# One add for up to four listed tiles in the second layer of a relational graph network

## The chip, the cores and the metric

One Trainium2 chip, one of its cores. The metric is the time of one execution on the device in microseconds, as the median of the timed runs. The engines are named as in the profile: PE (matmuls; PEld are its weight loads), DVE (vectors), ACT (activations), POOL (here the engine that issues the gathers), SP (other DMAs). A name with q behind it is an engine's sequencer.

## The reference

A graph of 12500 nodes with 128 features and 200000 edges, sorted by their target `dst`, each of one of 10 relations. Two layers follow one another, then comes a layer norm over the sum with the input.

```python
def _rgcn_layer(x, src, dst, edge_type, w_rel, root, bias):
    N = x.shape[0]
    seg = dst * NUM_REL + edge_type
    xs = x[src]
    sums = jax.ops.segment_sum(xs, seg, num_segments=N * NUM_REL)
    cnt = jax.ops.segment_sum(jnp.ones(seg.shape, x.dtype), seg, num_segments=N * NUM_REL)
    mean = (sums / jnp.maximum(cnt, 1.0)[:, None]).reshape(N, NUM_REL, -1)
    return jnp.einsum('nrd,rdo->no', mean, w_rel) + x @ root + bias
...
edge_type = jnp.argmax(msg[:, NODE_EMB_DIM:-NODE_EMB_DIM], axis=1).astype(jnp.int32)
h = jax.nn.relu(_rgcn_layer(x, src, dst, edge_type, w_rel1, root1, b1))
return _rgcn_layer(h, src, dst, edge_type, w_rel2, root2, b2)
...
x = _layernorm(x + _L0_gnn_ref(x, node_vec, edge_weight, edge_attr_42, ...), axis=-1)
```

## The kernel before

The edges are cut into 1563 tiles of 128. For a tile, POOL gathers the 128 rows of its sources by an indirect DMA (`gathered`, L814); DVE makes a one-hot matrix of 128 edges by w nodes, in which an edge has its weight, 1/cnt, in the column of its target relative to the tile's first node (`hots`, L821); PE multiplies the two, which gives a sum of 128 features by w nodes in PSUM; and DVE adds it to a wide array in SBUF, at the column of the first node. That column is only known on the chip, so the address comes from a register.

**Layer 1** (`layer_1`) walks all tiles with 120-column one-hots (12 nodes by 10 relations; matmul L1058, add L847). While it runs, rows of h that are finished go into the gathered table, so that later tiles can sum the part of layer 2 whose sources are finished. Those sums are kept in `SD`, and the "heavy" blocks of layer 2 begin with them.

**Layer 2** (`layer_2`, L1382) has two kinds of tiles. First come 177 plain tiles, in 45 bunches of up to four; their one-hots are 12 wide, of `keyE` and `wE`. Then come 678 *listed* tiles: the edges whose source was not finished yet in layer 1, picked out and brought together by `brought_together` and `listed` (L1313) in six lists of up to 128 tiles, while the plain tiles run. `listed` turns the list on PE, makes for each tile its first node (`bB`), the gather's indices (`idxB`), the one-hots' columns (`keyB`) and weights (`wB`), and compares each tile's reach with its width by `by_tile` (L1340 and L1341: one pair of instructions for each step of the width in the list). A reach beyond the width sets a flag, and the call then goes through the general loops behind layer 2. The first nodes go from `biB` (L1346) through a DMA of ACT to the row `rowB`.

Listed tiles are sparser in nodes: a tile needs a window of 14 to 119 nodes (`width2`, in steps). They form two walks, listed tiles 0 to 488 (dense, 112 then 14 to 26 wide) and 489 to 677 (26 to 119 wide). `units` (L1384) makes bunches of up to four tiles of the same width in each walk, 182 in all: 157 of four, 9 of three, 7 of two, 9 of one. `taken_in_turns` (L1397) merges the walks: the first 40 and the last 40 tiles are of the first walk, and between them bunches of the second are taken as a running account allows, which counts 3 x width for each tile.

The loop over the bunches p sets the order on every engine. It does, for bunch p: the one-hots of bunch p+3 (`AH` = 3); the gathers of p and its matmuls (L1570) into PSUM bank p, out of five (`zy` three, `zq` two); then the adds of bunch p-2 (`BE` = 2), L1599, one for each tile:

```python
s = acc2[:, ds(offs[second, t], w)]
nc.vector.tensor_tensor(s, s, zps[q][:, j * w:(j + 1) * w], op=ALU.add)
```

`offsets` (L825, its load is L832) fetches the addresses of eight tiles by one register load of DVE's sequencer. Six buffers of eight tiles hold the gathered rows, so that POOL may be some 41 to 48 tiles ahead of PE's matmuls. Between the bunches stand, in every 12 tiles, 20 matmuls of 256 columns for a heavy block (`seen`, L1486, the tile `alone`) and their add three tiles later (L1494); and, as soon as all tiles of a block of 256 nodes are added, its `finish` (L1498): PE turns the block (L1504), DVE and ACT normalise it (`normed`, L754 to L764), SP stores it. 51 blocks are finished, the last three behind the last tile.

Of the kernel before, what the change touches and what calls it, by code (L numbers as in the profile page):

```python
# [20 lines left out]
P = 128  # L21
# [3 lines left out]
WN = 12  # L25
KW = NREL * WN
WMAX = 120
G = 16
QB = 4
GB = 6  # L30
# [37 lines left out]
def rgcn_resnorm_kernel(ctx: ExitStack, tc: tile.TileContext, x, src, dst, attr, w_rel1, root1, b1,  # L68
# [120 lines left out]
    def width2(u):  # L189

        a, b = rows_at(u, extent[u >= UX])
        w = max(row_width(r) for r in range(a, b + 1))
        assert w <= WMAX
        return w

    const = ctx.enter_context(tc.tile_pool(name="const", bufs=1))
    dram = ctx.enter_context(tc.tile_pool(name="dram", bufs=1, space=DRAM))
# [624 lines left out]
                                    op0=ALU.is_equal, op1=ALU.mult)  # L822
        return oh

    def offsets(row, t0, n, limits, ring=True):  # L825

        lims = [limits(t0 + j) for j in range(n)]
# [4 lines left out]
        vals = nc.values_load_multi_w_load_instructions(  # L832
            row, engines=[DVE], min_val=min(a for a, _ in lims), max_val=max(b for _, b in lims),
            skip_runtime_bounds_check_because="clamped to these nodes on the chip")[1]
        return [nc.s_assert_within(v, a, b, skip_runtime_bounds_check_because="clamped to these nodes on the chip")
                for v, (a, b) in zip(vals, lims)]
# [476 lines left out]
    def listed(c):  # L1313
# [20 lines left out]
        bi = comp.tile([P, 1], I32, name="biB")  # L1334
# [11 lines left out]
        nc.vector.tensor_scalar(bi[:p], b[:p, 0:1], -1.0, float(TOPN), op0=ALU.mult, op1=ALU.add)  # L1346
# [4 lines left out]
        nc.vector.tensor_copy(idxB[:, u0:u0 + p], ps[:, :p])  # L1351
# [30 lines left out]
    def layer_2():  # L1382

        def units(a, b):  # L1384
            u, r = a, []
            while u < b:
                w = width2(u)
                n = 1
                while u + n < b and n < min(QB, YB // w) and width2(u + n) == w:
                    n += 1  # L1390
                r.append((True, u, n, w))
                u += n
            return r
# [136 lines left out]
        for p in range(-AH, NB + BE):  # L1530
# [21 lines left out]
            if p < NB:  # L1552
# [14 lines left out]
                    gs[j] = g, at  # L1567
                for j in range(n):
                    g, at = gs.pop(j)
                    nc.tensor.matmul(zp[:, j * w:(j + 1) * w], g[:, at * C:(at + 1) * C], oh[:, j * w:(j + 1) * w],  # L1570
                                     start=True, stop=True)
                i = issued[p + 1]
            if flag is None and i >= NG - 28 * QB:
                assert not jobs.due
# [8 lines left out]
                    seen_in(j)  # L1583
            for q in [q for q in sorted(zps) if q <= p - (1 if p >= NB - 4 else BE)]:
                second, t0, n, w = bunches[q]
                for j in range(n):
                    t = t0 + j
                    if (second, t) not in offs:
                        if second:
                            m = min(GB2, (UX if t < UX else NT2) - t)  # L1590
                            assert {t // P, (t + m - 1) // P} <= ready
                            vals = offsets(rowB[:, t:t + m], t, m, bounds2, False)
                        else:
                            m = min(GB2, (NX if t >= T0 else T0) - t)
                            vals = offsets(rowP[:, t:t + m], t, m, bounds, False)
                        offs = {k: v for k, v in offs.items() if k[0] and (k[1] >= UX) != (t >= UX)}
                        offs.update({(second, t + d): v for d, v in enumerate(vals)})
                    s = acc2[:, ds(offs[second, t], w)]
                    nc.vector.tensor_tensor(s, s, zps[q][:, j * w:(j + 1) * w], op=ALU.add)  # L1599
                del zps[q]  # L1600
# [176 lines left out]
```

## Time and profile before

| | us |
|---|---|
| median of the 3 timed runs | 3716.18 |
| fastest and slowest of them | 3711.78, 3717.28 |
| the profiled execution | 3674.72 |
| its span, from the first instruction to the last | 3672.9 |

| engine | busy us | share of the span |
|---|---|---|
| PE | 2278.8 | 62% |
| PE's weight loads | 1884.6 | 51% |
| DVE | 2042.8 | 56% |
| ACT | 514.7 | 14% |
| POOL | 2293.4 | 62% |

The first gather of layer 2 starts at 2358.2 us; the first listed tile is gathered at 2639.9 us, the last at 3629.3 us. A group's row reads: line, engine, operation, written <- read tiles, shape and number of instructions, then busy us and the mean ns of one, then the engine's idle time just before them and what ended most of it ("remote" is a releaser that the trace doesn't name). A row of a timeline has its start, its length, the instruction and, in brackets, the idle time ahead of it. The mean granted clock of PE in this execution was 0.747.

### The profile page before, as it was taken

How to read it: one execution, taken by the hardware profiler on the slowest of the kernel's cores; microseconds unless marked ns; L12 is line 12 of the kernel's file. 1: busy time of each engine (PE TensorE's matmuls, PEld its weight loads, DVE VectorE, ACT ScalarE, POOL GpSimd, SP SyncE). 2: the span in 40 equal slices, each digit the busy share in tenths (PEclk: the TensorE clock that was granted, in tenths of full speed). 3: DMA queues.
4: the chain of work that ended last, by engine and by line, in shares of the span. 5: the costliest groups of instructions: out<-in, count | busy, mean ns of one | idle time of the engine just before them, and what ended most of it. 6: DMA issues, size and time to landing. Idle time of an engine off the chain costs nothing.

```text
span 3672.9 us, 39395 instructions
## 1 busy us (share of the span) xinstructions
PE 2278.8 (62%) x11107; PEld 1884.6 (51%) x11107; DVE 2042.8 (56%) x6834; ACT 514.7 (14%) x799; POOL 2293.4 (62%) x2430
## 2 busy tenths in 40 slices
PE   1557676767676767666667677633556567666533
PEld 0445555555555655555555555523455456555533
DVE  4646576767565756575656565438653234333344
ACT  1111121212121212121212121100000000000000
POOL 5664666666666666666666666566566666666663
PEclk7677887888888888888888877855667666776655
DMA  4553655455555555555555555531234444444321
GB/s 121 156 166 100 191 158 189 151 190 160 187 165 176 171 171 174 170 173 174 178 174 174 161 162 160 149 82 52 70 103 138 134 132 145 141 145 133 86 61 43
DMA packets 377189, 529.35 MB, mean 144 GB/s; under 512 B 56664, under 2 KB 284467, under 8 KB 376964
## 3 DMA queue, kind: packets, MB, share of 16 engines
q0 software_dynamic: 99552, 249.45, 23.7%
q1 hardware_dynamic: 249209, 264.48, 22.2%
q10 hardware_dynamic: 28203, 12.82, 1.2%
q8 instruction: 92, 1.51, 0.2%
q14 instruction: 133, 1.09, 0.1%
HBM read 372.75 MB, written 160.19 MB: 145 GB/s over the span
## 4 chain that ended last, share of the span: by engine, by line
PE 18%; DVE 12%; issue 11%; another core or an unknown queue 9%; POOL 1%; DVEq 1%; ACT 1%; DMA 0%; SPq 0%; POOLq 0%; ACTq 0%
PE alone L807 5%; PE zp L1058 4%; DVE oh L821 3%; DVE cc L1599 3%; PE zy L1570 2%; PE pf L807 2%; PE yb L915 2%; POOL g L814 1%; PE zq L1570 1%; DVE cc L847 1%; DVEq L832 1%; DVE cc L1261 1%; PE pf L1296 1%; DVE go L1249 0%
## 5 line engine op out<-in xcount | busy, mean ns | idle before, releaser
L814 POOL DMA_INDIRECT g<-XH,idxE x1386 | 1313.9, 948 | 737.8 <-issue 364.9
L1058 PEld LDWEIGHTS zp<-oh,g 128*128 128x128 f32 x5898 | 901.9, 230 | 399.0 <-DVE cc L847 177.1
L1058 PE MATMUL zp<-oh,g 128*128 128x120 f32 x5898 | 943.4, 317 | 238.5 <-DVE cc L847 135.2
L847 DVE TENSOR_TENSOR cc<-cc,zp 128x240 f32 (+1 forms) x1563 | 606.5, 388 | 791.3 <-remote 317.6
L814 POOL DMA_INDIRECT g<-YD,idxB x678 | 641.9, 947 | 348.8 <-issue 193.2
L915 PE MATMUL yb<-w,a 128*128 128x512 f32 (+1 forms) x576 | 347.9, 694 | 343.4 <-ACT ys L921 176.7
L821 DVE TENSOR_SCALAR oh<-bank,keyE,wE 128x120 f32<-128x120 f32 x1563 | 517.5, 393 | 0.0
L807 PE MATMUL alone<-cc,w 128*128 128x256 f32 (+2 forms) x920 | 302.9, 498 | 93.9 <-issue 64.1
L1570 PE MATMUL zy<-oh,g 128*128 128x12 f32 (+20 forms) x1158 | 217.6, 324 | 198.7 <-DVE cc L1599 124.2
L921 ACT ACTIVATE ys<-yb 128x512 f32<-128x512 f32 (+2 forms) x291 | 153.0, 526 | 1325.4 <-remote 534.1
L1570 PEld LDWEIGHTS zy<-oh,g 128*128 128x128 f32 x1158 | 222.4, 278 | 210.7 <-DVE cc L1599 128.4
L807 PEld LDWEIGHTS alone<-cc,w 128*128 128x128 f32 x920 | 233.7, 270 | 147.3 <-issue 75.5
L915 PEld LDWEIGHTS yb<-w,a 128*128 128x128 f32 x576 | 110.6, 239 | 377.6 <-ACT ys L921 198.3
L807 PE MATMUL pf<-cc,w 128*128 128x256 f32 (+2 forms) x1040 | 247.1, 395 | 17.1 <-issue 8.3
L814 POOL DMA_INDIRECT g<-in_x_dram,idxE x177 | 167.6, 947 | 134.9 <-PE zp L1058 62.6
L814 POOL DMA_INDIRECT g<-YD,idxE x177 | 168.4, 951 | 114.7 <-issue 59.7
L807 PEld LDWEIGHTS pf<-cc,w 128*128 128x128 f32 x1040 | 205.3, 211 | 50.8 <-issue 15.7
L776 ACT ACTIVATE cc<-zero 128x1280 f32<-128x1280 f32 x170 | 214.5, 1262 | 0.0
L1599 DVE TENSOR_TENSOR cc<-cc,zy 128x12 f32 (+22 forms) x579 | 102.5, 177 | 181.1 <-remote 87.9
L821 DVE TENSOR_SCALAR oh<-columns,keyB,wB 128x15 f32<-128x15 f32 (+26 forms) x678 | 159.6, 319 | 0.0
L754 DVE TENSOR_TENSOR cc<-pf,x 128x256 f32<-128x256 f32 (+2 forms) x52 | 21.2, 408 | 227.2 <-remote 94.2
L1570 PE MATMUL zq<-oh,g 128*128 128x15 f32 (+26 forms) x552 | 98.6, 319 | 63.6 <-issue 28.4
(257 smaller groups left out, 1567.8 us busy)
## 6 DMA issues: line engine op xcount, KB each, us to landing
SD<-cc SPq DMA_DIRECT2D x41, 1280.0 KB
cc<-SD SPq DMA_DIRECT2D x41, 1280.0 KB
YD<-ys SPq DMA_DIRECT2D x194, 256.0 KB
m<-in_edge_attr_dram SPq DMA_DIRECT2D x48, 672.0 KB
g<-XH,idxE POOLq DMA_INDIRECT x1386
YD<-ys SPq DMA_DIRECT2D x97, 128.0 KB
XH<-hb SPq DMA_DIRECT2D x44, 256.0 KB
g<-YD,idxB POOLq DMA_INDIRECT x678
```

The costliest lines, as they stand in the source:

```text
L776: nc.scalar.activation(cc[:, l, h * H:(h + 1) * H, o:o + n], zero[:, None, :n].to_broadcast([P, H, n]), AF.Copy)
L807: nc.tensor.matmul(po[:, :n], wsb[l][:, r, :], sums[:, r], start=(r == 0), stop=(w is None and r == NREL - 1))
L814: nc.gpsimd.indirect_dma_start(out=g[:, j * C:(j + n) * C], out_offset=None, in_=table, in_offset=bass.IndirectOffsetOnAxis(ap=idx, axis=0))
L821: nc.vector.tensor_scalar(oh[:, j * m:(j + 1) * m], cols[:, :m], keys[:, j:j + 1], weights[:, j:j + 1], op0=ALU.is_equal, op1=ALU.mult)
L832: vals = nc.values_load_multi_w_load_instructions(row, engines=[DVE], min_val=min(a for a, _ in lims), max_val=max(b for _, b in lims), sk ...
L847: nc.vector.tensor_tensor(s, s, z, op=ALU.add)
L915: nc.tensor.matmul(yb[:h, :m], fin_a[k][:, b * P:b * P + h], wsb[1][:, r:r + m // C, :], start=True, stop=True)
L921: nc.scalar.activation(ys[:h, :m], yb[:h, :m], AF.Copy)
L1058: nc.tensor.matmul(zp[:, o + l * KW:o + (l + 1) * KW], g[:, (slot[j] + l) * C:(slot[j] + l + 1) * C], oh[:, j * KW:(j + 1) * KW], start=Tr ...
L1261: nc.vector.copy_predicated(to[:, c - m:EW - m], go[:, c - KW:], a[:, c:])
L1570: nc.tensor.matmul(zp[:, j * w:(j + 1) * w], g[:, at * C:(at + 1) * C], oh[:, j * w:(j + 1) * w], start=True, stop=True)
L1599: nc.vector.tensor_tensor(s, s, zps[q][:, j * w:(j + 1) * w], op=ALU.add)
```

## The change

The listed tiles of a walk are put together in groups of four, two or one (`group_at`), and a group is a bunch. A group of n tiles has one window: its width is a constant (38.6 for four, 20.8 for two) over the smallest density of its rows, rounded up with some nodes on top, at most 120; where four tiles need more, two are tried, then one. A group doesn't cross a list. All one-hots of the group are as wide as the window, relative to the group's first node. The matmuls of its tiles write the same columns of PSUM, one on top of the other, and **one** DVE add brings the sum to SBUF. One register load brings the addresses of up to eight groups of the same size (`alike`), with a stride of n in `rowB`.

The 678 listed tiles then make 216 bunches (141 of four, 39 of two, 36 of one). Widths are 45 to 119 in the groups of four, 28 to 118 in those of two; the mean width of a one-hot goes from 27 to 68 columns. Pairs are the listed tiles from 572 to 645 with a few others, singles those from 646 on; both stand between groups of four of the first walk.

`listed` now needs the first node of a group instead of a tile's. PE turns the 128 values to a row, DVE takes the greatest of each group (in reversed order, so the first node) and writes it to all tiles of the group, writes `rowB` from that row itself, and PE turns the row back into a column. For this two more `yield`s stand in each list, that is two more pieces that are placed between bunches; the DMA of ACT goes.

```diff
+GROUPS = ((4, 38.6), (2, 20.8))
...
+    def group_at(u, end):
+
+        for n, m in GROUPS:
+            if u % P + n <= P and u + n <= end:
+                a, b = rows_at(u, extent[u >= UX])[0], rows_at(u + n - 1, extent[u >= UX])[1]
+                if a:
+                    w = int(m / min(dense[a * RT:(b + 1) * RT]) + 2.99)
+                    if w <= WMAX:
+                        return n, w
+        return 1, width2(u)
...
-        nc.vector.tensor_scalar(bi[:p], b[:p, 0:1], -1.0, float(TOPN), op0=ALU.mult, op1=ALU.add)
-        nc.scalar.dma_start(rowB[:, u0:u0 + p], bi[:p])
-        key = comp.tile([P, P], F32, name="keyb")
+        nc.tensor.transpose(ps[0:1, P:P + p], b[:p, 0:1], ident[:p, :p])
+        yield 1
...
+        for a, n, m in runs:
+            to = firsts[:, a:a + m * n]
+            if n == 1:
+                nc.vector.tensor_copy(to, ps[0:1, P + a:P + a + m])
+            else:
+                nc.vector.tensor_reduce(lasts[:, :m], ps[0:1, P + a:P + a + m * n].rearrange("p (m n) -> p m n", n=n), axis=AX.X, op=ALU.max)
+                nc.vector.tensor_copy(to.rearrange("p (m n) -> p m n", n=n), lasts[:, :m, None].to_broadcast([1, m, n]))
+        nc.tensor.matmul(ps[:p, 2 * P:2 * P + 1], firsts[:, :p], ident[0:1, 0:1], start=True, stop=True)
+        nc.vector.tensor_scalar(rowB[:, u0:u0 + p], firsts[:, :p], -1.0, float(TOPN), op0=ALU.mult, op1=ALU.add)
+        yield 1
+        nc.vector.tensor_copy(b[:p, 0:1], ps[:p, 2 * P:2 * P + 1])
         nc.vector.tensor_scalar(key[:p], si[:p], -1.0, b[:p, 0:1], op0=ALU.mult, op1=ALU.add)
...
-        by_tile(b[:, 2:3], [width2(u) - 0.5 for u in range(u0, u0 + p)])
+        by_tile(b[:, 2:3], [width_of[u] - 0.5 for u in range(u0, u0 + p)])
...
-                owed = min(owed + u[2] * (mean - 3 * u[3] - 125), mean)
+                owed = min(owed + u[2] * (mean - 3 * u[3] / u[2] - 125), mean)
...
-                    nc.tensor.matmul(zp[:, j * w:(j + 1) * w], g[:, at * C:(at + 1) * C], oh[:, j * w:(j + 1) * w],
-                                     start=True, stop=True)
+                    o = 0 if second else j * w
+                    nc.tensor.matmul(zp[:, o:o + w], g[:, at * C:(at + 1) * C], oh[:, j * w:(j + 1) * w],
+                                     start=not second or j == 0, stop=not second or j == n - 1)
...
-                for j in range(n):
+                for j in range(1 if second else n):
...
-                            m = min(GB2, (UX if t < UX else NT2) - t)
+                            step, m = n, alike[t]
...
-                            vals = offsets(rowB[:, t:t + m], t, m, bounds2, False)
+                            vals = offsets(rowB[:, t:t + m * n:n], t, m, bounds2, False, n)
```

DVE's order in the middle of the listed stage, before: the one-hots of the bunch three ahead (here of 16 columns, four in one row), then an address calculation of the sequencer ("ISA") and an add for each of the four tiles of the bunch two back.

```order
L821 TENSOR_SCALAR oh_95<-columns,keyB,wB 128x16 x4
L1599 ISA
L1599 TENSOR_TENSOR cc<-cc,zy_15678 128x16
L1599 ISA
L1599 TENSOR_TENSOR cc<-cc,zy_15678 128x16
L1599 ISA
L1599 TENSOR_TENSOR cc<-cc,zy_15678 128x16
L1599 ISA
L1599 TENSOR_TENSOR cc<-cc,zy_15678 128x16
```

The same engine in the same part of the program after it, where groups of four of the first walk alternate with single tiles of the second.

```order
L846 TENSOR_SCALAR oh_98<-columns,keyB,wB 128x51 x4
L1636 ISA
L1636 TENSOR_TENSOR cc<-cc,zy_15680 128x74
L846 TENSOR_SCALAR oh_92<-columns,keyB,wB 128x74
L1636 ISA
L1636 TENSOR_TENSOR cc<-cc,zq_17203 128x51
L846 TENSOR_SCALAR oh_93<-columns,keyB,wB 128x52 x4
L1636 ISA
L1636 TENSOR_TENSOR cc<-cc,zq_17204 128x74
L846 TENSOR_SCALAR oh_94<-columns,keyB,wB 128x84
L1636 ISA
L1636 TENSOR_TENSOR cc<-cc,zy_15678 128x51
```

Four pairs of address and add have become one for each group; a single tile has a one-hot, an address and an add of its own, and takes a whole turn of the loop.

DVE's order in a list, from the reduction to each tile's greatest node on (L1343), before; `biB` is what ACT's DMA takes to `rowB`, and the rows of L832 and L1599 are those of a plain bunch that follows.

```order
L1343 TENSOR_REDUCE bB<-si 128x1
L1344 TENSOR_SCALAR bB<-bB,reach_173,reach_172 128x1
L1346 TENSOR_SCALAR biB<-bB 128x1
L1349 TENSOR_SCALAR keyb<-si,bB 128x128
L832 TENSOR_LOAD rowP
L1599 ISA
L1599 TENSOR_TENSOR cc<-cc,zy_15680 128x12
```

After it, in the first list: these rows stand one bunch later than the reduction, behind the turning on PE (`pf` is its result). The first two rows belong to `brought_together`.

```order
L1315 TENSOR_SCALAR go<-columns,fB 127x7
L1317 TENSOR_TENSOR cc<-columns,go 127x896
L1384 COPY keyb<-pf 1x2
L1386 TENSOR_REDUCE dn<-pf 1x31
L1387 COPY keyb<-dn 1x124
L1386 TENSOR_REDUCE dn<-pf 1x1
L1387 COPY keyb<-dn 1x2
L1389 TENSOR_SCALAR rowB<-keyb 1x128
L1636 ISA
```

The column for the keys comes one bunch later again, as a copy of PE's second result, and only then the keys (L1392, before it L1349).

More of the change, by code (lines that the diff above doesn't have):

```diff
@@ L194, in width2 @@
         return w
+    def group_at(u, end):
[7 more added lines that the diff above has]
+        return 1, width2(u)
+    groups2, u = [], 0
+    while u < NT2:
+        n, w = group_at(u, UX if u < UX else NT2)
+        groups2.append((u, n, w))
+        u += n
+    alike = {}
+    for k, (u, n, _) in enumerate(groups2):
+        m = 1
+        while m < GB2 and k + m < len(groups2) and groups2[k + m][1] == n and (groups2[k + m][0] < UX) == (u < UX):
+            m += 1
+        alike[u] = m
+    width_of = {u + j: w for u, n, w in groups2 for j in range(n)}
     const = ctx.enter_context(tc.tile_pool(name="const", bufs=1))
@@ L823, in hots, with offsets @@
         return oh
-    def offsets(row, t0, n, limits, ring=True):
-        lims = [limits(t0 + j) for j in range(n)]
+    def offsets(row, t0, n, limits, ring=True, step=1):
+        lims = [limits(t0 + j * step) for j in range(n)]
         if ring:
@@ L1333, in listed @@
         b = comp.tile([P, 4], F32, name="bB")
-        bi = comp.tile([P, 1], I32, name="biB")
+        key = comp.tile([P, P], F32, name="keyb")
+        firsts, lasts = key[0:1], dn[0:1]
         def by_tile(to, vals):
@@ L1345, in listed @@
                                 op0=ALU.max, op1=ALU.min)
-        nc.vector.tensor_scalar(bi[:p], b[:p, 0:1], -1.0, float(TOPN), op0=ALU.mult, op1=ALU.add)
-        nc.scalar.dma_start(rowB[:, u0:u0 + p], bi[:p])
-        key = comp.tile([P, P], F32, name="keyb")
+        nc.tensor.transpose(ps[0:1, P:P + p], b[:p, 0:1], ident[:p, :p])
+        yield 1
+        runs = []
+        for u, n, _ in groups2:
+            if u0 <= u < u0 + p:
+                if runs and runs[-1][1] == n:
+                    runs[-1][2] += 1
+                else:
+                    runs.append([u - u0, n, 1])
+        for a, n, m in runs:
+            to = firsts[:, a:a + m * n]
+            if n == 1:
+                nc.vector.tensor_copy(to, ps[0:1, P + a:P + a + m])
+            else:
+                nc.vector.tensor_reduce(lasts[:, :m], ps[0:1, P + a:P + a + m * n].rearrange("p (m n) -> p m n", n=n), axis=AX.X, op=ALU.max)
[4 more added lines that the diff above has]
+        nc.vector.tensor_copy(b[:p, 0:1], ps[:p, 2 * P:2 * P + 1])
         nc.vector.tensor_scalar(key[:p], si[:p], -1.0, b[:p, 0:1], op0=ALU.mult, op1=ALU.add)
@@ L1384, in units @@
         def units(a, b):
[L1385 to L1393, printed above, removed]
+            return [(True, u, n, w) for u, n, w in groups2 if a <= u < b]
         walks = [units(0, UX), units(UX, NT2)]
@@ L1589, in layer_2 @@
                         if second:
-                            m = min(GB2, (UX if t < UX else NT2) - t)
-                            assert {t // P, (t + m - 1) // P} <= ready
-                            vals = offsets(rowB[:, t:t + m], t, m, bounds2, False)
+                            step, m = n, alike[t]
+                            assert {t // P, (t + m * n - 1) // P} <= ready
+                            vals = offsets(rowB[:, t:t + m * n:n], t, m, bounds2, False, n)
                         else:
+                            step = 1
                             m = min(GB2, (NX if t >= T0 else T0) - t)
@@ L1596, in layer_2 @@
                         offs = {k: v for k, v in offs.items() if k[0] and (k[1] >= UX) != (t >= UX)}
-                        offs.update({(second, t + d): v for d, v in enumerate(vals)})
+                        offs.update({(second, t + d * step): v for d, v in enumerate(vals)})
                     s = acc2[:, ds(offs[second, t], w)]
```

## The prediction

> **What bounds the kernel now.** I read the busy time by stretches first, because the share of an engine over the whole span is a mean over stages. In each row below stand the stretch, its length, and the busy time of PE, PE's weight loads, DVE, ACT and POOL with the number of their instructions.
>
> ```profile
> core 0: us, PE busy (x) PEld busy (x) DVE busy (x) ACT busy (x) POOL busy (x), PEclk, DMA share, GB/s
> ...
> 1600.00:2100.00 500.00, 339.28 (x1837) 275.75 (x1837) 307.78 (x858) 103.81 (x143) 323.16 (x341) 0.85 0.55 171
> ...
> 2600.00:2760.00 160.00, 100.20 (x423) 85.08 (x423) 93.70 (x436) 7.13 (x18) 90.96 (x96) 0.69 0.32 92
> ...
> 2960.00:3460.00 500.00, 328.23 (x1380) 284.26 (x1380) 188.07 (x913) 18.06 (x49) 327.37 (x346) 0.69 0.46 135
> 3460.00:3630.00 170.00, 59.15 (x275) 55.52 (x273) 60.66 (x307) 2.66 (x9) 114.51 (x122) 0.52 0.23 60
> 3630.00:3673.00 43.00, 19.82 (x85) 17.88 (x85) 24.40 (x119) 2.06 (x7) 0.22 (x1) 0.50 0.13 26
> ```
>
> POOL's gathers are one to a tile. 500/341 = 1.466 us each in layer 1, with DVE busy 62% of the time; 500/346 = 1.445 us in the listed stage, with DVE at 38%; 170/122 = 1.393 us near its end, with PE at 35% and DVE at 36%. DVE's and PE's load hardly move this pace, so POOL sets it. Only 2600:2760, where the lists are made (160/96 = 1.67 us), and the last 43 us, with one gather left, go by something else. The timeline of POOL shows how the pace comes about; in brackets is the idle time before a gather.
>
> ```profile
> 3024.74 0.95 POOL L814 DMA_INDIRECT g<-YD,idxB  x1 [3.50 <-PE pf L1504]
> ...
> 3047.95 0.94 POOL L814 DMA_INDIRECT g<-YD,idxB  x1 [3.46 <-PE zy L1570]
> ...
> 3059.61 0.95 POOL L814 DMA_INDIRECT g<-YD,idxB  x1 [1.96 <-PE zy L1570]
> ...
> 3533.44 0.94 POOL L814 DMA_INDIRECT g<-YD,idxB  x1 [4.35 <-remote]
> 3567.68 0.95 POOL L814 DMA_INDIRECT g<-YD,idxB  x1 [4.54 <-remote]
> ```
>
> 16 gathers lie between the first two rows (23.21 us, 1.451 each), 8 to the third (11.66 us, 1.458), 24 between the last two (34.24 us, 1.427). Without the pause a gather starts (23.21 - 0.95 - 3.46) / 15 = 1.253 us after the one before. The pause grows with the number of gathers before it, 2.0, 3.5 and 4.5 us, so 8, 16 or 24 at a stretch come to nearly the same pace. A stretch ends where eight buffers aren't known to be free. That depends on PE, which stands behind DVE:
>
> ```profile
> L754 DVE TENSOR_TENSOR cc<-pf,x 128x256 f32<-128x256 f32 x42 | 17.8, 424 | 210.0 <-remote 89.6 <-PE zy L1570 70.6 <-issue 23.9
> L1494 DVE TENSOR_TENSOR cc<-cc,alone 128x256 f32<-128x256 f32 x41 | 17.2, 418 | 134.1 <-remote 86.9 <-PE zy L1570 22.4 <-PE zq L1570 15.0
> ```
>
> From 2700 on, DVE idles 344 us before the 42 finished blocks and the 41 sums of the finished part, both of which need PE. It is not short of time there.
>
> **The change, part by part.** 678 listed tiles keep 678 gathers, 678 one-hots and their matmuls. Their adds become 216 (141 groups of four, 39 of two, 36 of one), the loads of their addresses 33 instead of 86.
>
> ```profile
> L821 DVE TENSOR_SCALAR oh<-columns,keyB,wB 128x15 f32<-128x15 f32 x85 | 19.2, 313 | 0.0
> ...
> L821 DVE TENSOR_SCALAR oh<-columns,keyB,wB 128x66 f32<-128x66 f32 x9 | 2.5, 356 | 0.0
> L1599 DVE TENSOR_TENSOR cc<-cc,zy 128x119 f32 x9 | 2.5, 278 | 10.1 <-DVE cc L1599 4.5 <-issue 3.8 <-remote 1.8
> ...
> L1599 DVE TENSOR_TENSOR cc<-cc,zq 128x66 f32 x8 | 1.8, 224 | 13.3 <-PE alone L807 8.9 <-remote 2.3 <-issue 1.9
> ```
>
> ```profile
> L832 DVEq TENSOR_LOAD <-rowB x86: 309/599/2106, 2705.7 to 3660.7; - x86
> ```
>
> *Beside POOL.* One add in a run takes 0.2 us (a row of the tail, below), so 462 fewer are 92 us; 53 fewer loads at 0.599 are 32 us. One-hots widen from a mean of 27 to 68 columns: at most 2.5/9 - 19.2/85 = 0.05 us each, 34 us. The 216 adds are 74 wide in the mean, between 224 and 278 ns, about 0.05 us more each: 11 us. DVE is relieved of 92 + 32 - 34 - 11 = 79 us. POOL's pace hides all of it, as 1600:2100 against 2960:3460 shows; without that cover it would be the gain of the first rival.
>
> *The steady stage: -6.* What DVE's relief can do is lengthen POOL's stretches. The last sum of a finished part is this row, and from there on the pauses come every 24 gathers instead of 16:
>
> ```profile
> 3495.37 0.29 DVE L1494 TENSOR_TENSOR cc<-cc,alone 128x128 f32<-128x128 f32 x1 [9.10 <-remote]
> ```
>
> ```profile
> L814 POOL DMA_INDIRECT g<-YD,idxB x577: 942/947/1023, 2760.7 to 3601.8; - x193
> ```
>
> So fewer stops of DVE do lengthen them, at 1.451 - 1.427 = 0.024 us a gather. From the first to the last of these 577 gathers go 841.1 us, 1.460 each; at 1.427 throughout that is -19, the near end. I take 250 gathers at -0.024, for the groups of four that follow one another at both ends of the stage (about 200 tiles) and a few more. The far end, +60, is the second rival's mechanism.
>
> *The lists: +8.* These groups are from 2600:2760, where all six lists are made:
>
> ```profile
> L1341 DVE TENSOR_TENSOR bB<-bB 128x1 f32<-128x1 f32 x30 | 4.9, 162 | 1.7 <-DVE bB L1340 0.5 <-issue 0.2
> L1340 DVE TENSOR_SCALAR bB<-place 128x1 f32<-128x1 f32 x30 | 4.6, 153 | 1.5 <-DVE bB L1341 0.7
> ...
> L1351 DVE CAST idxB<-pf 128x128 int32<-128x128 f32 (+1 forms) x6 | 1.6, 269 | 7.5 <-remote 5.8 <-PE zy L1570 1.7
> ...
> L1371 DVE COPY wB<-pf 128x128 f32<-128x128 f32 (+1 forms) x5 | 1.3, 268 | 4.5 <-PE pf L1369 4.5
> ...
> L1346 DVE TENSOR_SCALAR biB<-bB 128x1 int32<-128x1 f32 (+1 forms) x6 | 0.9, 152 | 0.2
> ```
>
> The steps of width grow from 30 pairs to 46: 32 x 0.158 = 5.1 us. 24 copies and reductions of one row, six addresses and six columns come, six L1346 go: 30 more in all, between 30 x 0.15 and 30 x 0.27, 4.5 to 8 us. Two more places per list at which DVE waits for PE: L1351 and L1371 waited 12.0 us in 11 cases, 1.1 each, so 12 x 1.1 = 13 us. Behind such a wait stand the next bunch's one-hots and the adds that free PE's banks, and PE waits for both. Together 23 to 26 us of DVE, in a stretch where DVE is idle for 66 of 160 us, and where POOL is 160 - 96 x 1.451 = 21 us behind its pace. Nothing (all in the idle time) and +25 (all in line) are the ends; I take a third. A gain is unlikely: of what goes, only six short instructions and six DMA issues of ACT, which is busy for 7 of 160 us.
>
> *The tail: -11.* After the last gather DVE goes on by itself.
>
> ```profile
> 3613.13 0.18 DVE L1599 TENSOR_TENSOR cc<-cc,zy 128x23 f32 x1 [2.01 <-remote]
> 3613.83 0.18 DVE L1599 TENSOR_TENSOR cc<-cc,zy 128x23 f32 x1 [0.52 <-DVE cc L1599]
> ...
> 3629.96 0.18 DVE L1599 TENSOR_TENSOR cc<-cc,zy 128x23 f32 x1 [6.60 <-remote]
> ...
> 3640.86 0.81 DVE L1599 TENSOR_TENSOR cc<-cc,zy 128x24 f32 x4
> ```
>
> ```profile
> L821 DVE TENSOR_SCALAR oh<-columns,keyB,wB 128x26 f32<-128x26 f32 (+1 forms) x27 | 6.1, 293 | 0.0
> ...
> L1599 DVE TENSOR_TENSOR cc<-cc,zy 128x25 f32 (+3 forms) x26 | 4.7, 180 | 11.3 <-remote 6.6 <-DVE cc L1599 3.8
> ...
> L1599 DVE TENSOR_TENSOR cc<-cc,zq 128x25 f32 (+3 forms) x22 | 3.9, 179 | 2.0 <-DVE cc L1599 1.5
> ```
>
> ```profile
> L832 DVEq TENSOR_LOAD <-rowB x6: 309/598/702, 3638.7 to 3660.7; - x6
> ```
>
> Four adds take 0.81 us there. The 26 + 22 adds become 13: 35 x 0.2 = 7.0 us less, 13 x 0.05 = 0.7 more for width; four loads at 0.598 go, 2.4 less; 27 one-hots widen, 27 x 0.05 = 1.3 more. That is -7.4. The rows at 3613 to 3630 show, while POOL still issues, single adds that wait 0.5 to 6.6 us, some of them for the add just before. With one add for four tiles DVE has fewer such waits ahead of the last gather: 0 to -8, of which I take -3.6. Ends of the tail: 0 (the closing blocks' chain of PE, DVE and ACT keeps the end) and -16.
>
> *Sum.* 8 - 6 - 11 = -9 us. Against the profiled execution, 3674.72 us (span 3672.9), that is 3665.7. The median of the timed runs, 3716.18, lies 41.5 us above that execution; the 9 us taken from it give **3707 us**.
>
> **The rivals.** *First, faster: DVE's loop with PE is what holds POOL* (0.13). For it: DVE's single adds above wait for each other while POOL issues, and a group has one. Then the steady stage gets its -19, the lists give back 16 of their 21 us, the tail -16: -51, 3665. More would need pauses to vanish altogether (576 x 0.2 = 115 us more), and layer 1's 1.466 with its different load on DVE and PE speaks against it. The Trainium skill, "Perfetto Trace Analysis", section "Optimizing Scalar/DVE Operations", says that grouping into larger operations can raise throughput if the engine is saturated; DVE's 38% in 2960:3460 is not that case.
>
> *Second, slower: the bunch shrinks* (0.25). One-hots are made three bunches ahead, PE has five banks, one to a bunch. Before, a bunch holds 678/182 = 3.7 tiles, after it 678/216 = 3.1, and where the two walks alternate (some 477 tiles in 163 bunches) 2.9: when DVE stands before a finished block, PE has 8 to 9 tiles to go on with instead of 11. POOL needs 8. Falling from 16 to 8 at a stretch costs only 0.007 a gather, 3 us; a pause that truly waits for PE costs more:
>
> ```profile
> 2879.92 0.95 POOL L814 DMA_INDIRECT g<-YD,idxB  x1 [5.28 <-PE zy L1570]
> ...
> 2955.20 0.95 POOL L814 DMA_INDIRECT g<-YD,idxB  x1 [6.60 <-PE zq L1570]
> ```
>
> Both end stretches of 8 and are 3.3 and 4.6 us over the 1.96 above. With 60 pauses in the 477 tiles and one in eight late, 7.5 x 4 = 30 us, and +30 + 8 - 11 = +27: 3743. It decides from about three late pauses on (12 us, against 17 of tail and stretches). Against it: DVE has less to do between its stops.
>
> *Third, slower: the lists in line* (0.12). All 25 us show: 25 - 6 - 11 = +8, 3724.
>
> *Fourth, slower: wide one-hots hold POOL up* (0.03). If a one-hot kept a gather from being made, 678 x 0.05 us times POOL's busy 0.65 would add 22 us: 22 + 8 - 11 = +19, 3735. In layer 1 one-hots of 120 columns run beside gathers that take no longer:
>
> ```profile
> L814 POOL DMA_INDIRECT g<-XH,idxE x1386 | 1313.9, 948 | 737.8 <-issue 364.9
> ...
> L821 DVE TENSOR_SCALAR oh<-bank,keyE,wE 128x120 f32<-128x120 f32 x1563 | 517.5, 393 | 0.0
> ```
>
> The mean is 948 ns beside 120 columns, the median 947 in the listed stage, beside 27. The Trainium skill has such a rule in "SBUF — State Buffer", section "Who interferes with whom": a tensor_scalar in a two-port mode locks GpSimd out of the shared ports and so starves descriptor generation; these rows show no sign of it.
>
> *Fifth, it doesn't do what it says* (0.02): if a group's nodes don't fit its window, the flag sends the call through the general loops, and the time is far above all of this.
>
> **How the numbers follow.** The forecast has 0.45; its own ends, +7 and -25, put 0.30 on faster and 0.15 on no change. 0.2%, or 7.4 us, is about what a measurement of this kernel can tell from none. Faster: 0.30 + 0.13 = 0.43. Same: 0.15 + 0.03 of the second rival + 0.05 of the third = 0.23. Slower: 0.22 + 0.07 + 0.03 + 0.02 = 0.34. The range goes from 3678 (two thirds of the way from the forecast to the first rival's 3665, with some 0.08 left below) to 3745 (the second rival's price, with 0.10 left above).
>
> **What would show it.** Right: the gathers of 2960:3460 stay within 340 to 352; pauses come every 24 gathers where fours follow fours; the last gather is followed by about 32 us instead of 43, with some 13 adds; DVE's busy time in the listed stage falls by about 79 us and POOL's pace doesn't follow. Wrong: more than 355 gathers in 500 us (first rival); POOL's idle time with pauses over 5 us in the middle, released by PE (second); under 92 gathers in the stretch in which the lists are made (third); gathers longer than 0.95 us (fourth).

## The result, and the profile after

The change took 3685.99 us (median of 10 runs, 3682.37 to 3700.1), the kernel before 3707.98 us (median of 10, 3702.23 to 3717.28): a ratio of 0.9946, with a 95% interval of 0.9931 to 0.996, so 0.5% or some 20 us faster. Forecast were 9 us, from 3716 us, the median of three runs; over ten runs that kernel takes 3708 us, so the forecast time of 3707 us is practically that of the kernel before.

The two profiled executions don't show this by their spans: 3681.0 us after, 3672.9 before. Layer 1, in which not one instruction is changed, ends (first gather of layer 2) at 2385.4 us after and at 2358.2 us before. The profile of before is of an execution 1.1% below its timed runs, as the prediction noted. So only layer 2 is compared: 3672.9 - 2358.2 = 1314.7 us before, 3681.0 - 2385.4 = 1295.6 us after, 19 us less.

The stretches of the kernel after, with the same columns as in the prediction:

```profile
core 0: us, PE busy (x) PEld busy (x) DVE busy (x) ACT busy (x) POOL busy (x), PEclk, DMA share, GB/s
2600.00:2760.00 160.00, 95.52 (x390) 80.87 (x390) 96.10 (x407) 7.37 (x17) 90.62 (x96) 0.67 0.29 81
2960.00:3460.00 500.00, 319.45 (x1350) 271.28 (x1351) 157.22 (x683) 19.45 (x51) 324.55 (x344) 0.70 0.46 135
3460.00:3630.00 170.00, 71.50 (x363) 67.63 (x362) 56.67 (x252) 2.95 (x10) 112.64 (x120) 0.56 0.26 68
3653.00:3681.00 28.00, 11.86 (x53) 10.52 (x52) 14.81 (x63) 1.77 (x6) 1.36 (x2) 0.50 0.23 37
```

In 500 us of the listed stage DVE is busy for 157 us instead of 188, with 683 instructions instead of 913, and POOL makes 344 gathers instead of 346. DVE's relief is there and POOL's pace doesn't follow it. What is shorter is the end: from the last gather to the last instruction 3681.0 - 3653.7 = 27.3 us, against 3672.93 - 3629.28 = 43.7.

Where did DVE's saved time go? These are the adds of the listed tiles and the two other places at which DVE stops, from 2840 to 3620 us before, with busy time, mean and idle time ahead of them:

```profile
L1599 DVE TENSOR_TENSOR cc<-cc,zy 128x15 f32 (+20 forms) x320 | 58.6, 183 | 98.3 <-issue 33.5 <-remote 32.7 <-DVE cc L1599 25.3
L1599 DVE TENSOR_TENSOR cc<-cc,zq 128x15 f32 (+21 forms) x219 | 41.0, 187 | 63.9 <-remote 16.3 <-issue 14.2 <-DVE cc L1599 14.1
L754 DVE TENSOR_TENSOR cc<-pf,x 128x256 f32<-128x256 f32 (+2 forms) x38 | 15.8, 417 | 194.0 <-remote 76.4 <-PE zy L1570 69.1 <-issue 23.9
L1494 DVE TENSOR_TENSOR cc<-cc,alone 128x256 f32<-128x256 f32 (+2 forms) x38 | 15.3, 403 | 122.9 <-remote 74.2 <-PE zy L1570 22.4 <-PE zq L1570 17.6
```

And from 2840 to 3640 us after, where the add is L1636, the finished block L779 and the sum of the finished part L1529:

```profile
L1636 DVE TENSOR_TENSOR cc<-cc,zy 128x119 f32 (+28 forms) x109 | 25.2, 231 | 82.6 <-remote 45.7 <-issue 22.9 <-PE zq L1606 10.6
L1636 DVE TENSOR_TENSOR cc<-cc,zq 128x48 f32 (+27 forms) x74 | 16.9, 229 | 59.7 <-remote 41.2 <-issue 10.7 <-PE zy L1606 6.7
...
L779 DVE TENSOR_TENSOR cc<-pf,x 128x256 f32<-128x256 f32 (+2 forms) x39 | 16.2, 417 | 184.6 <-remote 122.3 <-PE zy L1606 20.7 <-PE zq L1606 20.4
L1529 DVE TENSOR_TENSOR cc<-cc,alone 128x256 f32<-128x256 f32 (+2 forms) x39 | 15.8, 405 | 185.4 <-remote 64.0 <-PE zq L1606 38.2 <-PE zy L1606 28.9
```

The adds' busy time falls from 99.6 to 42.1 us. The idle time ahead of them falls only from 162 to 142 us, although there are 183 instead of 539 of them, and that ahead of the sums (L1529) grows from 123 to 185 us, in a stretch that is 20 us longer. What DVE is spared has become waiting, one instruction further on. That the rows name PE does not mean that PE was still at work; the end of the next section shows what these waits are.

### The profile page after: what moved, and what is told of

Same layout as the page of the kernel before. It is cut to its first block, busy times and chain, and to the rows that moved or that the text cites. A ratio compares the mean times of both kernels' runs of the same rounds, so it can differ in the third digit from the quotient of the medians.

```text
span 3681.0 us, 38527 instructions
## 1 busy us (share of the span) xinstructions
PE 2315.0 (63%) x11125; PEld 1905.6 (52%) x11125; DVE 1995.4 (54%) x6434; ACT 513.6 (14%) x799; POOL 2287.7 (62%) x2430
## 4 chain that ended last, share of the span: by engine, by line
PE 16%; issue 12%; another core or an unknown queue 9%; DVE 9%; POOL 4%; ACT 1%; DMA 1%; DVEq 0%; POOLq 0%; ACTq 0%
POOL g L839 4%; PE alone L832 4%; PE zp L1083 4%; DVE oh L846 3%; PE zy L1606 2%; PE yb L940 1%; PE pf L832 1%; PE zq L1606 1%; DVE cc L1636 1%; DVE cc L1286 1%; PE pf L1539 1%; DVE cc L872 1%; DVE go L1274 0%; ACT cc L801 0%
## 5 line engine op out<-in xcount | busy, mean ns | idle before, releaser
L1083 PEld LDWEIGHTS zp<-oh,g 128*128 128x128 f32 x5898 | 931.5, 236 | 407.9 <-issue 187.9
L1083 PE MATMUL zp<-oh,g 128*128 128x120 f32 x5898 | 974.2, 324 | 232.1 <-DVE cc L872 127.9
L940 PE MATMUL yb<-w,a 128*128 128x512 f32 (+1 forms) x576 | 366.2, 727 | 373.2 <-ACT ys L946 214.6
L832 PE MATMUL alone<-cc,w 128*128 128x256 f32 (+2 forms) x920 | 286.1, 475 | 88.3 <-issue 62.2
L1606 PE MATMUL zy<-oh,g 128*128 128x12 f32 (+30 forms) x1168 | 225.9, 344 | 154.7 <-DVE cc L1636 100.4
L832 PEld LDWEIGHTS alone<-cc,w 128*128 128x128 f32 x920 | 222.6, 257 | 137.8 <-issue 72.7
L832 PE MATMUL pf<-cc,w 128*128 128x256 f32 (+2 forms) x1040 | 243.3, 390 | 17.9 <-DVE cc L872 8.5
L832 PEld LDWEIGHTS pf<-cc,w 128*128 128x128 f32 x1040 | 202.1, 208 | 51.8 <-issue 16.8
L846 DVE TENSOR_SCALAR oh<-columns,keyB,wB 128x45 f32<-128x45 f32 (+35 forms) x678 | 176.4, 334 | 0.0
L1636 DVE TENSOR_TENSOR cc<-cc,zy 128x12 f32 (+24 forms) x306 | 59.1, 193 | 164.4 <-remote 95.7
L1606 PE MATMUL zq<-oh,g 128*128 128x45 f32 (+33 forms) x542 | 101.9, 333 | 64.8 <-issue 57.0
L1606 PEld LDWEIGHTS zq<-oh,g 128*128 128x128 f32 x542 | 100.0, 258 | 73.1 <-issue 61.8
```

The lines of the kernel that those rows point to most:

```text
L832: nc.tensor.matmul(po[:, :n], wsb[l][:, r, :], sums[:, r], start=(r == 0), stop=(w is None and r == NREL - 1))
L846: nc.vector.tensor_scalar(oh[:, j * m:(j + 1) * m], cols[:, :m], keys[:, j:j + 1], weights[:, j:j + 1], op0=ALU.is_equal, op1=ALU.mult)
L940: nc.tensor.matmul(yb[:h, :m], fin_a[k][:, b * P:b * P + h], wsb[1][:, r:r + m // C, :], start=True, stop=True)
L1083: nc.tensor.matmul(zp[:, o + l * KW:o + (l + 1) * KW], g[:, (slot[j] + l) * C:(slot[j] + l + 1) * C], oh[:, j * KW:(j + 1) * KW], start=Tr ...
L1606: nc.tensor.matmul(zp[:, o:o + w], g[:, at * C:(at + 1) * C], oh[:, j * w:(j + 1) * w], start=not second or j == 0, stop=not second or j = ...
```

## The experiments

In the tables below the stages run from gather to gather (the start of that gather of POOL), so that they hold the same tiles in every kernel: gathers 1563 to 1739 (counted from 0) are the plain tiles, 1740 to 2417 the listed ones. Each column is one traced execution.

**The halves of the change, on a chip on which the kernel before took 3709.5 us.** Four kernels ran there, beside the same 15 runs of the kernel before (3705.3 to 3717.87). In all of them bunches of several groups are possible:

```diff
+                    k = r[-1] if r else None
+                    if k and size_of[k[1]] == n and k[3] == w and k[2] + n <= min(QB, YB // w * n):
+                        r[-1] = (True, k[1], k[2] + n, w)
...
+                    z = size_of[t0] if second else 1
+                    o = j // z * w
...
+                for j in range(n // z):
+                    t = t0 + j * z
```

With this a group of one tile is what a tile was before, and a bunch holds up to four tiles of equal groups. First, groups at the end alone:

```diff
-            if u % P + n <= P and u + n <= end:
+            if u % P + n <= P and u + n <= end and 440 < u < UX:
```

> Groups of four are formed only of the last 48 tiles of the first walk (one add for four, wide one-hots); all other listed tiles are as before, an add each, in 182 bunches as before. Theory E (the gain lies behind the last gather): the time from the last gather to the end falls from 43.7 us to 27 to 32, and the whole is 12 to 16 us faster than before (ratio 0.9957 to 0.9968). Rival S (the relief of DVE speeds the whole listed stage up): at most 4 us faster (0.999 or above).

Measured: 3699.4 us, 0.9971 (0.9961 to 0.9981). Second, groups everywhere but there:

```diff
+            if u % P + n <= P and u + n <= end and not 440 < u < UX:
```

> The other half: groups as in the change everywhere except in the last 48 tiles of the first walk, which keep an add each; bunches of up to four tiles of equal groups. Theory E: the time behind the last gather stays at 40 to 45 us, the whole is 0 to 7 us faster than before (0.998 to 1.0). Rival S: 14 to 20 us faster (0.9946 to 0.996).

Measured: 3698.32 us, 0.9966 (0.9953 to 0.9979). Third, all groups, packed:

> The change, but groups of one or two tiles of equal width share a bunch of up to four tiles (177 bunches instead of 216; still 216 adds). Rival B (smaller bunches cost time, since one-hots and banks are counted in bunches): 5 to 25 us faster than the change, ratio to before 0.988 to 0.993. Theory E (POOL's pace doesn't depend on it): as the change, 0.993 to 0.996.

Measured: 3688.37 us, 0.994 (0.9927 to 0.9952). Fourth, the change's lists, no groups:

```diff
-GROUPS = ((4, 38.6), (2, 20.8))
+GROUPS = ()
```

> The change's way of making a list (its row turned on PE, addresses written by DVE, two pieces more), but no groups: 678 adds, 182 bunches and one-hots as wide as before. The prediction's term: 96 gathers take 5 to 15 us longer where the lists are made, the whole 3 to 12 us slower (1.001 to 1.003). Rival, after the result (the stretch of the lists was shorter in the change): 0 to 6 us faster (0.9984 to 1.0).

Measured: 3699.84 us, 0.9971 (0.9959 to 0.9983), outside both ranges.

The fourth is the surprise. All four kernels have the change's lists, and those alone are worth 0.3%, where the prediction had them cost time. So the other three are to be compared with the fourth, not with before: groups at the end alone -0.4 us, groups elsewhere alone -1.5 us, both -11.5 us. The medians of such runs are some 4 us uncertain (half the intervals, 0.1%), so the halves are not told apart by the medians, and they do not add up to the whole: by the medians neither half alone shows a gain, and why both together do is not settled. The stages of the four traces show more, with one execution each. Before and after stand beside them (us); their traces are of other calls:

| gathers | before | lists alone | end only | not at the end | all, packed | after |
|---|---|---|---|---|---|---|
| layer 1, to 1563 | 2358.2 | 2381.1 | 2378.1 | 2381.5 | 2381.1 | 2385.4 |
| 1563 to 1740 | 281.7 | 278.6 | 280.4 | 277.0 | 278.7 | 275.6 |
| 1740 to 1856 | 171.9 | 173.6 | 173.7 | 178.0 | 177.8 | 177.9 |
| 1856 to 2330 | 696.3 | 698.7 | 700.6 | 694.6 | 691.2 | 688.6 |
| 2330 to 2417 | 121.1 | 121.9 | 122.4 | 121.6 | 121.5 | 126.2 |
| last gather to the end | 43.7 | 44.6 | 39.6 | 43.7 | 36.9 | 27.3 |

Against the lists alone, the packed groups take 4.2 us more at the first listed tiles, 7.5 us less in the middle (691.2 - 698.7), and 0.4 + 7.6 us less from gather 2330 to the end. Together that is -11.3, near the medians' -11.5. Where no groups are at the end, the end stays (43.7 against 44.6); where groups are at the end alone, it is 5.0 us shorter and the middle is not. So the end's share comes from the adds at the end, and theory E holds in kind, but not its sizes: the end shrinks by 5 to 8 us, not by 12 to 16, and the kernel without groups at the end comes to 0.9966 and not to 0.998 or more. Rival S is not nothing either, with 3.7 us net for the stage from 1740 to 2417, but it missed its range for groups at the end alone (0.9971, where it had 0.999 or above).

The end itself, by DVE's one-hots and adds behind the last gather, in the lists alone (span 3698.4 us, from 3651 on):

```profile
L847 DVE TENSOR_SCALAR oh<-columns,keyB,wB 128x25 f32<-128x25 f32 (+1 forms) x31 | 7.0, 293 | 0.0
L1647 DVE TENSOR_TENSOR cc<-cc,zy 128x25 f32 (+3 forms) x30 | 5.4, 180 | 10.4 <-remote 4.7 <-issue 2.4 <-DVE cc L1647 2.4
...
L1647 DVE TENSOR_TENSOR cc<-cc,zq 128x25 f32 (+3 forms) x22 | 3.9, 179 | 2.0 <-DVE cc L1647 1.5
```

packed (from 3651 on):

```profile
L847 DVE TENSOR_SCALAR oh<-columns,keyB,wB 128x85 f32<-128x85 f32 (+2 forms) x25 | 6.4, 320 | 0.0
...
L1647 DVE TENSOR_TENSOR cc<-cc,zy 128x85 f32 (+2 forms) x6 | 1.4, 239 | 0.4 <-issue 0.2
L1647 DVE TENSOR_TENSOR cc<-cc,zq 128x78 f32 (+3 forms) x6 | 1.4, 226 | 0.8 <-DVE oh L847 0.5 <-DVE cc L1647 0.3
```

and after (from 3653 on):

```profile
L846 DVE TENSOR_SCALAR oh<-columns,keyB,wB 128x85 f32<-128x85 f32 (+1 forms) x17 | 4.4, 338 | 0.0
L1636 DVE TENSOR_TENSOR cc<-cc,zy 128x82 f32 (+1 forms) x6 | 1.4, 239 | 1.7 <-PE pf L1539 1.5 <-issue 0.2
L1636 DVE TENSOR_TENSOR cc<-cc,zq 128x78 f32 (+3 forms) x4 | 0.9, 224 | 0.4 <-DVE cc L1636 0.3
```

52 adds with 9.3 us of work and 12.4 us of idle time ahead of them become 12 with 2.8 and 1.2 us. In the change there are only 10 adds and 17 one-hots left, because POOL's last pause lies elsewhere. Packed, the last pause is 22 gathers before the last one, in the change 6 (both rows are the gather behind a pause, then the last gather of all):

```profile
3622.76 0.95 POOL L840 DMA_INDIRECT g<-YD,idxB  x1 [4.46 <-remote]
...
3650.30 0.94 POOL L840 DMA_INDIRECT g<-YD,idxB  x1 [0.30 <-issue]
```

```profile
3646.12 0.94 POOL L839 DMA_INDIRECT g<-YD,idxB  x1 [4.55 <-remote]
...
3653.73 0.94 POOL L839 DMA_INDIRECT g<-YD,idxB  x1 [0.30 <-issue]
```

In the packed trace DVE stands ahead of a finished block for 24.3 us, until 3655.34 us, which is 5.0 us behind the last gather, although PE had turned that block by 3631.6 us. In the trace of the change DVE comes out of such a wait at 3645.97 us, within POOL's last pause. So 4.7 of the 9.6 us by which the change's end is shorter than the packed one's were paid in the stage before it (126.2 against 121.5). Packed bunches of up to four tiles (177 instead of 216) end up at 0.994, the change at 0.9946, with intervals that overlap. That answers rival B as far as it goes: the smaller bunches cost nothing that shows, though by the two intervals a cost of up to some 9 us isn't excluded.

**Where the lists' 10 us come from: left open.** Two kernels were to split the change's lists: the kernel before with two more `yield 1` in each list and nothing else, and the change's lists, without groups, without their two extra `yield 1`. With them ran the kernel before and the change, unchanged, for their stages.

```diff
         key = comp.tile([P, P], F32, name="keyb")
+        yield 1
+        yield 1
         nc.vector.tensor_scalar(key[:p], si[:p], -1.0, b[:p, 0:1], op0=ALU.mult, op1=ALU.add)
```

> The kernel before with two more pauses between the pieces of each list, as many as the change has, and nothing else. Theory Y (the lists' gain of 0.3% comes from the work being spread over more bunches): 0.996 to 0.998. Theory D (it comes from the addresses, which no longer go through a DMA of ACT): 0.999 to 1.001.

And from the kernel with the lists alone:

```diff
         nc.tensor.transpose(ps[0:1, P:P + p], b[:p, 0:1], ident[:p, :p])
-        yield 1
...
         nc.vector.tensor_scalar(rowB[:, u0:u0 + p], firsts[:, :p], -1.0, float(TOPN), op0=ALU.mult, op1=ALU.add)
-        yield 1
```

> The change's way of making a list without its two extra pauses (turning to a row, addresses by DVE and turning back stand in one piece), no groups. Theory D: 0.996 to 0.998. Theory Y: 0.999 or slower, since DVE then waits for PE twice within a piece.

> The kernel before, once more, for the times of its stages on this chip. All theories: layer 1 ends, as in the runs of the change, at 2375 to 2390 us instead of the 2358 us of the first profile; what the stages of layer 2 take is then compared with the change.

> The change, once more. Theory E (the end): the time from gather 2350 to the end is again 8 to 14 us shorter than in the kernel before, and the time behind the last gather 27 to 38 us.

All four ran on another chip, and there the kernel before takes 3072.0 us (median of 23 runs), not 3710. Two more pauses: 3072.51 us, 0.9999 (0.999 to 1.0008). The lists without theirs: 3075.03 us, 1.0008 (0.9999 to 1.0017). The kernel before 3069.08 us, the change 3067.99 us (one run each); layer 1 ends at 1974.2 us there, and from gather 2350 to the end the change takes 101.1 us instead of 103.3, not 8 to 14 us less. The gathers don't pause on this chip, and the 0.3% that the two theories were to explain doesn't appear there. Two further runs of the first kernel met such chips again:

> Two more pauses between the pieces of a list, nothing else. Where the gathers pause, theory Y (spreading): 0.996 to 0.998; theory D (the addresses' way): 0.999 to 1.001. Where they don't pause: 0.999 to 1.001 by both.

> Two more pauses between the pieces of a list, nothing else; meant for a chip on which the gathers pause (3700 us in all). There, theory Y (spreading gives the lists' gain of 0.3%): 0.996 to 0.998; theory D (the addresses' way gives it): 0.999 to 1.001, and the stages of layer 2 then show, beside those of the run with the change's lists alone, where its 10 us are. On a chip without pauses it is 0.999 to 1.001 by both and leaves the question open.

Measured: 3070.46 us, 0.9996 (0.9987 to 1.0006), and 3070.15 us, 0.9995 (0.9986 to 1.0004). Neither Y nor D was tested where the 10 us appear. No trace of the kernel before from the chip of the four kernels exists either; in the table its stages of layer 2, from the faster execution, are within 3.1 us of those of the lists alone, and layer 2 as a whole is 2.7 us longer with the lists alone (1317.4 us) than before (1314.7). So 0.9971 is measured, and its place is not; that it lies in layer 1, which has the same instructions in all these kernels, isn't excluded.

**The change where gathers don't pause.** The kernel before and the change again, unchanged:

> The kernel before, for the times of its stages beside the change on one chip. Where the gathers pause (3700 us in all): layer 1 ends at 2375 to 2390 us, layer 2 takes 1320 to 1330 us. Where they don't (3070 us in all): as in the run before, 1974 and 1093 us.

> The change. Theory E and its rivals, where the gathers pause: 0.993 to 0.996, with layer 2 15 to 30 us shorter and layer 1 within 5 us. Where the gathers don't pause: POOL issues every 1.25 us up to the last one, so that all that can change is the end behind it, 19.6 us before: 0.998 to 1.0.

Measured: before 3068.97 us (one run), the change 3070.1 us against 3071.71 us (11 and 21 runs), 0.9999 (0.999 to 1.0008). The kernel before on that chip, first gathers near the end and then a stretch of the listed stage:

```profile
2899.10 0.94 POOL L814 DMA_INDIRECT g<-YD,idxB  x1 [0.30 <-issue]
2900.34 0.94 POOL L814 DMA_INDIRECT g<-YD,idxB  x1 [0.30 <-PE zy L1570]
2901.59 0.94 POOL L814 DMA_INDIRECT g<-YD,idxB  x1 [0.30 <-issue]
```

```profile
2300.00:2800.00 500.00, 370.89 (x1651) 320.93 (x1649) 223.23 (x1091) 22.13 (x61) 378.08 (x401) 0.74 0.56 167
```

The change there, the same stretch:

```profile
2300.00:2800.00 500.00, 373.83 (x1695) 322.20 (x1694) 201.74 (x879) 22.27 (x61) 378.09 (x400) 0.76 0.56 169
```

POOL issues a gather every 500/401 = 1.247 us, before and after, with DVE busy for 223 us or 202 us. The relief of DVE is the same kind as on the other chip, and it buys nothing in the listed stage: the whole stage is POOL's. The end behind the last gather is 19.5 us before and 17.7 us after (3067.2 - 3047.7, 3065.9 - 3048.2). DVE is hardly behind there when POOL is done: 7 adds are left before and 3 after, where the pausing chip leaves 48 and 10.

**What the waits on the pausing chip are.** On the chip without pauses, DVE's waits ahead of the sums of the finished part end with the matmuls that the sums need (`alone`). These are the rows from 2300 to 3040 us, before and then the change:

```profile
L1494 DVE TENSOR_TENSOR cc<-cc,alone 128x256 f32<-128x256 f32 (+2 forms) x41 | 16.6, 404 | 129.8 <-PE alone L807 129.7
```

```profile
L1529 DVE TENSOR_TENSOR cc<-cc,alone 128x256 f32<-128x256 f32 (+2 forms) x42 | 17.1, 406 | 188.1 <-PE alone L832 188.0
```

On the pausing chip the same rows name "remote" and matmuls of other tiles. The row of the prediction at 3495.37 us, with the last 20 matmuls that it needs, from the timeline of the kernel before:

```profile
3480.94 4.40 PE L807 MATMUL alone<-cc,w 128*128 128x128 f32 x20 [1.85 <-DVE cc L1494]
...
3495.37 0.29 DVE L1494 TENSOR_TENSOR cc<-cc,alone 128x128 f32<-128x128 f32 x1 [9.10 <-remote]
```

The matmuls ended at 3485.34 us, and DVE waited 10 us more. For all such waits of more than 1 us among the listed tiles, the time from the end of the last matmul to the start of the sum is:

| | waits | median us | longest us |
|---|---|---|---|
| before, pausing chip | 24 | 7.36 | 12.99 |
| change, pausing chip | 30 | 4.83 | 19.61 |
| before, chip without pauses | 26 | 0.04 | 0.11 |
| change, chip without pauses | 35 | 0.04 | 0.11 |

POOL's pauses don't wait for PE's work either, for the most part. By the kernel's order of the buffers, the first gather into a buffer overwrites the tile 41 places before it, so it has to wait for that tile's matmuls. In the kernel before, these had ended before the pause began in 36 of the 44 pauses of more than 1 us among the listed tiles (122 of 155 us), in the change in 37 of 46. The four longest pauses of before, 5.28 to 6.60 us, do wait for PE: each ends 0.27 us after those matmuls. So most of what POOL and DVE wait for on that chip is not work that PE still has to do, and relief of DVE doesn't shorten it. For DVE's sums it is a signal that comes late; for POOL's pauses it may also be something in POOL that the trace doesn't show. PE's mean granted clock is lower on that chip too (0.734 to 0.751 in its runs, against 0.788 to 0.801), but slower matmuls can't be the reason for a wait that goes on after they have ended.

## Why the prediction was right or wrong

**What bounds the kernel: right in the pace, wrong in one reason.** POOL's gathers set the pace. DVE's relief came as worked out: from the first listed gather to the end DVE is busy for 367.0 us instead of 414.1, and its register loads, which are the sequencer's and not in the busy time, take 52.4 us instead of 81.8. That is 76.5 us, where the prediction has 79. Even so POOL made 344 gathers in 500 us instead of 346 where it pauses, 400 instead of 401 where it doesn't. The first rival (DVE's loop with PE holds POOL) is thereby answered: waits for the add just before, 39 us in the two groups of before, are no longer among the main releasers, and POOL gains nothing by it. On chips without pauses the spacing of 1.25 us, which this rival would have needed, is there without any change to DVE. What doesn't hold is the prediction's reason for a pause, that it depends on PE, which stands behind DVE: in 36 of 44 pauses PE's work was done before.

**The tail, -11: right in kind.** 10 adds behind the last gather where the prediction had 13, and DVE's work there falls as it says. The size depends on where POOL's last pause falls: 5.0 us for groups at the end alone and 7.6 us packed; 17.3 us in the trace of the change (27.3 against 44.6), of which 126.2 - 121.9 = 4.3 us were paid just before. That the first two lie near the -7.4 worked out from the adds, loads and one-hots is in part luck: the packed end holds 5.0 us of a late signal, which that working doesn't have. The -3.6 taken for earlier progress is inside that scatter.

**The steady stage, -6: too large, and its sign is not certain.** From gather 1740 to 2417 it is 990.5 us packed and 992.7 us in the change, against 994.2 us in the lists alone: -3.7 and -1.5. Against the trace of before (989.4 us) there is no gain, and these are single executions. The saving is in the middle (-7.5 and -10.2), where the prediction put the loss by small bunches; the first 116 listed tiles, in which four-tile groups of 45 and 46 and then of 85 to 108 columns follow one another, lose some 4 us, where it expected a gain. The stretches of 24 gathers, by which the prediction had the gain come about, did not become more (4 before and after). What changed are the few pauses that did begin before PE's matmuls had ended: in the middle there are 5 of them with the lists alone (22 us in all) and 3 in the change (11 us); among the first 116 tiles there are 3 (13 us) and 6 (26 us).

**The lists, +8: wrong.** It is this step that failed: that a third of 23 to 26 us of added DVE work and waits would delay the gathers. The waits themselves came as forecast: ahead of the two new places in the lists (L1386 and L1391) DVE idles for 12.7 us in the change, where the prediction has 13. But the gathers don't show them. The plain tiles take 275.6 us instead of 281.7. In the change the lists are made among the first listed tiles too, the last at 2850 us, so the stage to look at goes from gather 1563 to 1856: 453.6 us before, 452.2 us with the lists alone, 453.5 us in the change. And the change's lists alone make the kernel 0.29% faster (0.9959 to 0.9983) where gathers pause. What gives that time is not known. That the stretch is hardly longer with them (452.2 to 456.5 us in all five kernels that have these lists) fits work that lies in time that was idle anyway; it doesn't say why the whole is faster. The third rival, all 25 us in line, falls with this step.

**The second rival (smaller bunches): not seen.** From gather 1856 to 2330 the change takes 688.6 us with its 216 bunches, the packed kernel 691.2 us with 177, and its longest pause there is 4.85 us. In 29 of its 32 pauses there PE had done what POOL needed before the pause began. **The fourth (wide one-hots hold POOL up): not seen**, since on the chip without pauses the spacing is the same with one-hots of 27 and of 68 columns.

So -9 was -20: from the kernel with the lists alone -10 where +8 was forecast, and from the groups -11 where -17 was. Half of the gain therefore comes from where the prediction had a loss. That the measured time still lies within the stated 3678 to 3745 us is owed to the width of that range, not to the sum.

## What to carry to other kernels

Work taken from an engine that waits for another comes back as a longer wait, except where the pace-setter has stopped: here it is the stretch behind the last gather that gains, on both kinds of chip. Before a wait is put down to the engine that the profile names, compare its end with the end of that engine's work; here they were often several us apart. Before a difference of 0.5% is explained from two profiles, compare a stage that the change doesn't touch; here it differed by 27 us. And a gain that lives in the pauses of one chip can be nothing on the next.

## What the runs showed of the hardware

The same kernel takes 3710 us on one chip and 3072 us on another (medians of 15 and 23 runs), although a gather takes the same 0.94 to 0.95 us on both and 1.25 us lie from one to the next where none pauses. On the slower chip POOL stops for some 2.0, 3.5 or 4.5 us after 8, 16 or 24 gathers, and layer 1 has its 1.47 us a gather from such pauses too, most of them after 4, 8 or 12 gathers; on the faster one it stops once in layer 2's first 177 tiles and never in the 678 listed ones.

On the slower chip signals between engines come late: DVE began a sum 7.4 us (median of 24 waits) after the last matmul that it needed, on the faster one 0.04 us (26 waits). That they come late because POOL issues gathers fits two things: of the 44 sums of before and after that began more than 1 us after those matmuls, 27 began within a pause of POOL, though the pauses are 16% of that time; and the pauses grow with the number of gathers before them. No run tests it. What makes one chip do this and not another was not tried either.
